# Edge terms on row groups, and four steps moved: n_h, the degrees' turn, a tap step and the first loads

## The chip, the cores and the metric

The kernel runs on one core of one Trainium2 chip. A core has TensorE (matrix products, results into eight PSUM banks), VectorE, ScalarE, GpSimd and SyncE; the profile calls them PE (PEld for its weight loads), DVE, ACT, POOL and SP. The metric is the device time of one execution in microseconds; lower is better. All data is float32.

## The reference, cut to what matters

x holds 128 graphs of 128 nodes with 256 channels. Layer 0 normalizes x and clips it at zero (h), and passes h through a gated network; layer 1 is a graph convolution over the first 25 nodes in five groups. What the change touches, cut from the reference:

```python
h = bn2(conv1d_17(relu(bn1(conv1(h)))))            # 17 taps along the nodes
x_conv = relu(h + xc)
s = x @ w_se.T + b_se                              # 3 numbers per node
sq = sum(s * s, axis=-1)
dist = sq[:, :, None] + sq[:, None, :] - 2.0 * einsum('bnd,bmd->bnm', s, s)
A = exp(-dist) * mask                              # mask: the graph's adjacency
msg = relu(x @ w_msg.T + b_msg)
x_nmp = einsum('bnm,bmd->bnd', A, msg)
x_in = concatenate([x_conv, x_nmp], axis=-1)
gi = x_in @ w_ih.T + b_ih
gh = x @ w_hh.T + b_hh
r, z = sigmoid(gi_r + gh_r), sigmoid(gi_z + gh_z)
nn_ = tanh(gi_n + r * gh_n)
out = (1.0 - z) * nn_ + z * x
# layer 1, for each of five groups of nodes
norm_adj = dinv[:, :, None] * (adj + I) * dinv[:, None, :]     # dinv: degree ** -0.5
out = relu(norm_adj @ (x @ W) + b)                             # twice
```

## The kernel before, in words

Work goes in 32 blocks of four graphs (BB = 4; 512 columns).

**Front, 0 to about 495 us.** The 17-tap convolution is done by spectra. weight_spectra (L155) turns the taps w2 into spectra in four steps per set, eight sets in all. One step is sixteen products with only 17 rows each (L162): the taps lie in four groups that start at partitions 0, 32, 64 and 96, so four products stand on four different row groups of the array and write to four banks. some_spectra (L361) does one such step wherever it is called. head_load, head_stats, head_norm, head_turn (transposes to ht, L209), head_conv1 (L223) and head_spectra (L238) bring the blocks of x to their spectra. constants (L119) computes the batch-norm factors: small operations on VectorE with a power on GpSimd, a broadcast bnb (L133), four products with the identity that spread it over the partitions (L136), a ScalarE copy bnr (L137) and the scaling of the weights wc1 (L138), which head_conv1 needs. Up to L391 every engine takes its instructions in the order of the code (manual_schedule, L350); after that only GpSimd and, for a while, SyncE do. spectral (L282) multiplies the spectra.

**Gates, about 495 to 1800 us.** For each block, beside_gates(i) (L950) is a generator whose steps prepare block i: messages (L512, its last three columns are s, put into lr), conv_out (L493, gives xc), edge_terms (L535), edges (L547), x_nmp (L558, gives xn). gate_inputs (L580) forms the sums t that the gates' seven-product scheme needs: of xc and ht on GpSimd, of xn on VectorE. gates(i) (L593) then runs four units of seven steps: r (from ht, xc, xn: six records of TensorE a step), n_h (from ht alone: two records), n_n (xc, xn: four), z (six). After each step it calls step() (L991), which advances the degrees' generator, and in every odd turn the preparation of block i + 1, in the other turns layer 1.

**Edges.** lr holds for each of the four graphs of a block 32 columns, of which five are used: 2s, -1 and -sq on the left side, s, sq and 1 on the right, so that five products per pair of nodes give -dist. edge_terms transposes both sides (L539); graph b's five rows then stand at partitions 32b to 32b + 4. It copies the left side to lt on ScalarE (L541), and on VectorE writes the right side into rt, 512 columns wide, with a mask bm (L543) that leaves in graph b's 128 columns only b's rows. One product of 128 rows and 512 columns (L552) gives all four graphs' -dist in one bank; one exp (L554) and one multiplication with the adjacency (L555) follow.

**Degrees.** degrees (L690) sums the adjacency's rows on VectorE, takes the power -0.5 in several steps, and then transposes the factors (L723), copies them (L725) and stores them (L726) in dvf and dvk. back_loads (L741) and prepare (L807) load them again, broadcast, for layer 1.

**Before the first block** the preparation of block 0 is done alone (L983), then its gate_inputs, then the loop over the blocks (L987).

PSUM is one pool of eight banks (L90), and bank() takes the next. SyncE's queue and ScalarE's queue issue the loads and stores.

Of the kernel before, what the change touches and what calls it, by code (L numbers as in the profile page):

```python
# [8 lines left out]
F32 = mybir.dt.float32  # L9
# [8 lines left out]
BB = 4  # L18
# [56 lines left out]
def gnn_kernel(ctx: ExitStack, tc: tile.TileContext, io, out0: bass.AP, out1: bass.AP):  # L75
# [43 lines left out]
    def constants():  # L119

        for j, v0 in enumerate((V_BN1, V_BN2)):
# [11 lines left out]
        nc.vector.tensor_copy(bnb, bn[:, 0].rearrange("p q c -> p (q c)")[:, :, None].to_broadcast([P, 2 * C, P]))  # L133
        psb = bank()
# [4 lines left out]
        nc.vector.tensor_add(brz, vec[:, V_IH:V_IH + 4], vec[:, V_HH:V_HH + 4])  # L139

# [199 lines left out]
    with front as es:  # L340
# [7 lines left out]
        with ExitStack() as ws:  # L348
# [6 lines left out]
            todo = [(c, q) for c in range(C) for q in range(D // WCH)]  # L355
            head_load(xk, ahead, 0, nc.scalar)
            nc.sync.dma_start(gt, io["gt"])
            taps = [taps_load(wp, *todo[0], nc.sync, split=4)]
# [23 lines left out]
            constants()  # L382
            some_spectra()
            head_stats(hk, 1)
            some_spectra()
            head_norm(1)
# [54 lines left out]
    def load(i):  # L441
# [9 lines left out]
        for b in range(BB):  # L451
# [31 lines left out]

    bm = cst.tile([P, BB], F32)
    nc.gpsimd.memset(bm, 1.0)
    nc.gpsimd.affine_select(out=bm, in_=bm, compare_op=ALU.is_ge, fill=0.0, base=0,
                            pattern=[[-32, BB]], channel_multiplier=1)
    nc.gpsimd.affine_select(out=bm, in_=bm, compare_op=ALU.is_ge, fill=0.0, base=31,
                            pattern=[[32, BB]], channel_multiplier=-1)

# [44 lines left out]
    def edge_terms(i):  # L535

        ps = bank()
        for k in range(2):
            nc.tensor.transpose(ps[:, k * P:(k + 1) * P], lr[:, k].rearrange("p b r -> p (b r)"), ident)  # L539
        lt = wk.tile([P, P], F32, tag="lt", name="lt", bufs=2)  # L540
        nc.scalar.copy(lt, ps[:, :P])  # L541
        rt = wk.tile([P, BB, N], F32, tag="rt", name="rt", bufs=1)
        nc.vector.tensor_tensor(rt, ps[:, None, P:2 * P].to_broadcast([P, BB, N]),  # L543
                                bm[:, :, None].to_broadcast([P, BB, N]), op=ALU.mult)
        lrs[i] = lt, rt

    def edges(i):  # L547

        at, _, _ = loaded.pop(i)
        lt, rt = lrs.pop(i)  # L550
        pd = bank()
        nc.tensor.matmul(pd, lt, rt.rearrange("p b n -> p (b n)"), start=True, stop=True)  # L552
        e = wk.tile([P, BB, N], F32, tag="e", name="e", bufs=1)
        nc.scalar.activation(e.rearrange("p b n -> p (b n)"), pd, AF.Exp)  # L554
        nc.vector.tensor_mul(e, e, at)  # L555
# [24 lines left out]
    def gate_inputs(i):  # L580

        tt = []
# [570 lines left out]
```

## Time and profile before

| | |
|---|---|
| three executions | 1921.88, 1923.89, 1928.10 us; median 1923.89 |
| the profiled execution | 1930.41 us, its span 1928.7 us |
| TensorE busy | 1900.0 us, 99% of the span |
| TensorE's mean clock | 0.992 of full |
| VectorE, ScalarE, GpSimd busy | 1288.2, 712.2, 610.3 us |
| L552, the edge product | 32 of 128x512 |
| one block of the gates without layer 1 | 37.15 us (725.11 to 762.26 in the chain of waits) |

All rows under the first are of the one profiled execution. A product of float32 is two records in the profile (L552 has 64 records for 32 products). Products overlap, so a record's own length (0.59 us for L552) is longer than the time by which it moves the next one; the chain of waits shows that time. "<-" behind an idle time names what ended it. Clock is the share of full speed that TensorE was granted.

### The profile page before, as it was taken

The page shows a single profiled execution, that of the slowest core. Times are in us where ns is not written, and L with a number is a line of the kernel's source. Part 1 is how long each engine was busy: PE and PEld are TensorE (multiplying, and loading weights), DVE is VectorE, ACT ScalarE, POOL GpSimd, SP SyncE. Part 2 cuts the span into 40 slices and gives each one's busy share as a digit, 9 for nine tenths or more (in the row PEclk, how much of TensorE's full clock was granted, in tenths as well). Part 3 has the DMA queues.
Part 4 walks back from the last instruction along what each step waited for, and adds up shares of the span by engine and source line. Part 5 has one row for each costly group of instructions (what it writes and reads, how often), then busy time and mean ns, then how long its engine had stood idle before and what let it go on. Part 6 is the DMA issues. An engine that isn't in the chain of part 4 may idle for free.

```text
span 1928.7 us, 29906 instructions
## 1 busy us (share of the span) xinstructions
PE 1900.0 (99%) x10418; PEld 1654.8 (86%) x10418; DVE 1288.2 (67%) x3247; ACT 712.2 (37%) x1459; POOL 610.3 (32%) x681
## 2 busy tenths in 40 slices
PE   8999999999999999999999999999999999999998
PEld 7888888988788888888888888888888888888887
DVE  6566547854687777877665677777656677787643
ACT  4453114411333343343343443334343433334334
POOL 1012541256234333433322233433322233343300
PEclk9899999999999999999999999999999999999999
DMA  8686987369842333233234433233234533222135
GB/s 310 256 317 231 304 286 254 133 227 305 273 117 72 72 91 80 74 94 107 71 89 100 131 88 94 72 72 114 79 86 94 150 72 101 70 72 74 35 93 150
DMA packets 248869, 265.76 MB, mean 138 GB/s; under 512 B 106866, under 2 KB 223943, under 8 KB 244239
## 3 DMA queue, kind: packets, MB, share of 16 engines
q1 hardware_dynamic: 236783, 196.74, 36.6%
q10 hardware_dynamic: 11936, 67.11, 9.0%
q8 instruction: 83, 1.36, 0.3%
q14 instruction: 67, 0.55, 0.1%
HBM read 178.66 MB, written 85.14 MB: 137 GB/s over the span
## 4 chain that ended last, share of the span: by engine, by line
PE 88%; DMA 5%; DVE 4%; POOL 1%; issue 1%; ACT 1%; SPq 0%; ACTq 0%; POOLq 0%; DVEq 0%
PE bank L613 43%; PE bank L314 6%; PE bank L519 5%; PE bank L933 5%; PE bank L873 5%; PE bank L223 4%; PE bank L309 3%; PE bank L565 3%; PE bank L501 3%; PE bank L238 3%; PE bank L162 2%; PE bank L552 1%; PE bank L504 1%; DMA v<-vd 1%; PE bank L852 1%; PE bank L784 1%
## 5 line engine op out<-in xcount | busy, mean ns | idle before, releaser
L613 PE MATMUL bank<-t,sw 128*128 128x256 f32 x1152 | 291.1, 380 | 0.0
L626 POOL TENSOR_TENSOR u<-u,m 128x256 f32<-128x256 f32 x128 | 92.8, 725 | 594.2 <-ACT m L624 524.6
L613 PEld LDWEIGHTS bank<-t,sw 128*128 128x128 f32 x1152 | 215.7, 190 | 29.7 <-issue 2.3
L613 PE MATMUL bank<-t,wih 128*128 128x256 f32 x768 | 197.2, 379 | 0.0
L613 PEld LDWEIGHTS bank<-t,wih 128*128 128x128 f32 x768 | 143.4, 190 | 19.3 <-issue 0.5
L306 POOL TENSOR_TENSOR vs<-v 128x512 f32<-128x512 f32 x78 | 101.4, 1320 | 115.8 <-DMA v<-vd 54.1
L223 PE MATMUL bank<-wc,ht 128*128 128x256 f32 x512 | 121.0, 389 | 1.7 <-ACT ht L210 1.6
L519 PE MATMUL bank<-wms,ht 128*128 128x259 f32 x512 | 122.3, 381 | 0.0
L613 PE MATMUL bank<-t,whh 128*128 128x256 f32 x384 | 114.9, 381 | 0.0
L613 PE MATMUL bank<-xc,wih 128*128 128x256 f32 x384 | 114.7, 380 | 0.0
L933 PE MATMUL bank<-w,hh 128*125 128x256 f32 (+9 forms) x480 | 113.5, 380 | 1.0 <-DVE hh L878 1.0
L613 PE MATMUL bank<-xn,wih 128*128 128x256 f32 x384 | 114.3, 379 | 0.1
L223 PEld LDWEIGHTS bank<-wc,ht 128*128 128x128 f32 x512 | 97.8, 196 | 16.6 <-ACT ht L210 3.6
L613 PE MATMUL bank<-ht,whh 128*128 128x256 f32 x384 | 110.3, 381 | 0.0
L519 PEld LDWEIGHTS bank<-wms,ht 128*128 128x128 f32 x512 | 97.2, 190 | 14.6
L873 PE MATMUL bank<-ax,w 128*128 128x500 f32 (+8 forms) x416 | 107.0, 396 | 0.3 <-DMA w<-in_w_dram 0.3
L631 DVE TENSOR_TENSOR u<-bank,u 128x256 f32<-128x256 f32 x128 | 53.7, 419 | 73.6 <-PE bank L613 73.6
L193 POOL TENSOR_TENSOR rs<-ve,mhalf 128x4 f32<-128x4 f32 x32 | 32.3, 1008 | 222.3 <-DVE ve L191 222.3
L523 ACT ACTIVATE msg<-msg 128x512 f32<-128x512 f32 x64 | 40.3, 630 | 168.2 <-DVE msg L520 162.2
L304 DVE SCALAR_TENSOR_TENSOR s<-X 128x256 f32<-128x256 f32 x78 | 49.0, 631 | 80.0 <-PE bank L314 79.8
L933 PEld LDWEIGHTS bank<-w,hh 128*125 128x125 f32 (+9 forms) x480 | 84.2, 177 | 19.3 <-DVE hh L878 1.4
L653 ACT ACTIVATE nn<-nn,vec 128x512 f32<-128x512 f32 x64 | 46.2, 722 | 129.6 <-DVE nn L652 129.6
(191 smaller groups left out, 4287.4 us busy)
## 6 DMA issues: line engine op xcount, KB each, us to landing
v<-vd SPq DMA_DIRECT2D x80, 512.0 KB
vd<-sp ACTq DMA_DIRECT2D x8, 2560.0 KB
yd<-ys ACTq DMA_DIRECT2D x40, 512.0 KB
w<-in_w_dram SPq DMA_DIRECT2D x40, 512.0 KB
htd<-ht ACTq DMA_DIRECT2D x32, 512.0 KB
ht<-htd SPq DMA_DIRECT2D x32, 512.0 KB
ym<-yd SPq DMA_DIRECT2D x32, 512.0 KB
xt<-in_xT_dram SPq DMA_DIRECT2D x32, 512.0 KB
```

Source lines behind the costliest of these rows:

```text
L223: nc.tensor.matmul(pv[:, bb, :], ht[:, c, b * N:(b + 1) * N], wc1[:, c, :], start=c == 0, stop=c == C - 1)
L238: nc.tensor.matmul(ps[:, bb * 2 * LW:(bb + 1) * 2 * LW], h1[:, 2 * h + bb, c * P:(c + 1) * P], fd, start=True, stop=True)
L306: nc.gpsimd.tensor_tensor(vs, vr, vi, op=ALU.add)
L309: nc.tensor.matmul(p1[:, :D], a[:, c], vs[:, c], start=c == 0, stop=c == C - 1)
L314: nc.tensor.matmul(ps[:, k * D:(k + 1) * D], u[:, c], w[:, c], start=c == 0, stop=c == C - 1)
L501: nc.tensor.matmul(ps[:, b * N:(b + 1) * N], ym[:, b, o * P:(o + 1) * P], idm, start=b == 0, stop=False)
L519: nc.tensor.matmul(ps[:, :D + 3], ht[:, c, b * N:(b + 1) * N], wms[:, c, :], start=c == 0, stop=c == C - 1)
L565: nc.tensor.matmul(ps[:, b * N:(b + 1) * N], msg[:, b, c * P:(c + 1) * P], e[:, b, :], start=True, stop=True)
L613: nc.tensor.matmul(ps, w, d, start=n == 0, stop=n == len(pairs) - 1)
L626: nc.gpsimd.tensor_tensor(got["u4"], got["u2"], got["m5"], op=ALU.add)
L873: nc.tensor.matmul(pv[:, q - q0, :], w1s[k5 + g][:, c, q * P:(q + 1) * P], xv[:, c], start=c == 0, stop=c == C - 1)
L933: nc.tensor.matmul(ps[:n1, :D], hh[:, q, at:at + n1], w2s[k5 + g][:, q, :], start=q == 0, stop=q == HID // P - 1)
```

## The change

1. **Edges.** rt and the mask bm go. edge_terms copies both transposed sides in one ScalarE copy (lt, now 2 x 128 columns). edges makes four products, each with the five rows of one graph at partitions 32b and 128 columns, into four banks; exp is taken four times over 128 columns, and the multiplication with the adjacency twice over two graphs.
2. **First block's n_h.** For block 0 the preparation stops when edges is done. The sums of ht and xc are formed, and gates(0) begins with the n_h unit. Behind its sixth step the rest of the preparation (x_nmp) and the sums of xn follow. In the other units of block 0 the preparation of block 1 advances on two turns of three instead of every odd turn. n_h's steps in block 0 don't call step(), so the degrees aren't advanced in them. Other blocks keep their order.
3. **Degrees.** Between the factors and their transposes the generator yields eight times instead of three.
4. **Norms' constants.** constants becomes a generator with two halts: one behind bnb, one at the end. Between them stand two steps of the spectra and head_stats of block 1.
5. **First loads.** gt is issued from ScalarE's queue ahead of block 0 of x; SyncE's queue begins with the four loads of the first taps.

```diff
@@ -118,6 +118,6 @@
 
     def constants():
         for j, v0 in enumerate((V_BN1, V_BN2)):
             g, b, m, v = (vec[:, v0 + 2 * q:v0 + 2 * q + 2] for q in range(4))
             sc, sh = bn[:, j, 0, :], bn[:, j, 1, :]
@@ -131,12 +132,14 @@
 
         bnb = hc.tile([P, 2 * C, P], F32, name="bnb")
         nc.vector.tensor_copy(bnb, bn[:, 0].rearrange("p q c -> p (q c)")[:, :, None].to_broadcast([P, 2 * C, P]))
+        yield
         psb = bank()
         for q in range(2 * C):
             nc.tensor.matmul(psb[:, q * P:(q + 1) * P], bnb[:, q, :], ident, start=True, stop=True)
         nc.scalar.copy(bnr.rearrange("p q d -> p (q d)"), psb)
         nc.vector.tensor_mul(wc1, wc1, bnr[:, 0:1, :].to_broadcast([P, C, D]))
         nc.vector.tensor_add(brz, vec[:, V_IH:V_IH + 4], vec[:, V_HH:V_HH + 4])
+        yield
 
     fw = cst.tile([P, 5], F32)
 
@@ -353,9 +356,9 @@
             wp = ws.enter_context(tc.tile_pool(name="wp", bufs=1))
             ahead = 5
             todo = [(c, q) for c in range(C) for q in range(D // WCH)]
+            nc.scalar.dma_start(gt, io["gt"])
+            taps = [taps_load(wp, *todo[0], nc.sync, split=4)]
             head_load(xk, ahead, 0, nc.scalar)
-            nc.sync.dma_start(gt, io["gt"])
-            taps = [taps_load(wp, *todo[0], nc.sync, split=4)]
             spectra = []
 
             def some_spectra(k=1):
@@ -379,10 +382,12 @@
             head_norm(0)
             some_spectra()
             head_turn(hk, 0)
-            constants()
+            consts = constants()
+            next(consts)
             some_spectra()
             head_stats(hk, 1)
             some_spectra()
+            next(consts)
             head_norm(1)
             head_stats(hk, 2)
             some_spectra()
@@ -479,14 +484,6 @@
     nb2 = cst.tile([P, 5, C], F32)
     nc.vector.tensor_mul(nb2, vec[:, V_B2:V_B2 + 5 * C].rearrange("p (g c) -> p g c", c=C),
                          nw[:, :, None].to_broadcast([P, 5, C]))
-    bm = cst.tile([P, BB], F32)
-    nc.gpsimd.memset(bm, 1.0)
-    nc.gpsimd.affine_select(out=bm, in_=bm, compare_op=ALU.is_ge, fill=0.0, base=0,
-                            pattern=[[-32, BB]], channel_multiplier=1)
-    nc.gpsimd.affine_select(out=bm, in_=bm, compare_op=ALU.is_ge, fill=0.0, base=31,
-                            pattern=[[32, BB]], channel_multiplier=-1)
 
     A_s, xcs, xns, ts, msgs, outs, lrs, xts = ({} for _ in range(8))
 
@@ -537,22 +534,23 @@
         ps = bank()
         for k in range(2):
             nc.tensor.transpose(ps[:, k * P:(k + 1) * P], lr[:, k].rearrange("p b r -> p (b r)"), ident)
-        lt = wk.tile([P, P], F32, tag="lt", name="lt", bufs=2)
-        nc.scalar.copy(lt, ps[:, :P])
-        rt = wk.tile([P, BB, N], F32, tag="rt", name="rt", bufs=1)
-        nc.vector.tensor_tensor(rt, ps[:, None, P:2 * P].to_broadcast([P, BB, N]),
-                                bm[:, :, None].to_broadcast([P, BB, N]), op=ALU.mult)
-        lrs[i] = lt, rt
+        lt = wk.tile([P, 2, P], F32, tag="lt", name="lt", bufs=2)
+        nc.scalar.copy(lt.rearrange("p k n -> p (k n)"), ps[:, :2 * P])
+        lrs[i] = lt
 
     def edges(i):
 
         at, _, _ = loaded.pop(i)
-        lt, rt = lrs.pop(i)
-        pd = bank()
-        nc.tensor.matmul(pd, lt, rt.rearrange("p b n -> p (b n)"), start=True, stop=True)
+        lt = lrs.pop(i)
+        pd = [bank() for _ in range(BB)]
+        for b in range(BB):
+            g = slice(32 * b, 32 * b + 5)
+            nc.tensor.matmul(pd[b][:, :N], lt[g, 0, :], lt[g, 1, :], start=True, stop=True)
         e = wk.tile([P, BB, N], F32, tag="e", name="e", bufs=1)
-        nc.scalar.activation(e.rearrange("p b n -> p (b n)"), pd, AF.Exp)
-        nc.vector.tensor_mul(e, e, at)
+        for b in range(BB):
+            nc.scalar.activation(e[:, b, :], pd[b][:, :N], AF.Exp)
+            if b % 2:
+                nc.vector.tensor_mul(e[:, b - 1:b + 1, :], e[:, b - 1:b + 1, :], at[:, b - 1:b + 1, :])
         A_s[i] = e
 
     def x_nmp(i):
@@ -577,30 +575,31 @@
 
         return d[:, 0, :H], d[:, 0, H:], d[:, 1, :H], d[:, 1, H:]
 
-    def gate_inputs(i):
-
-        tt = []
-        for k, (d, eng) in enumerate(((xcs[i], nc.gpsimd), (xns[i], nc.vector), (hts[i], nc.gpsimd))):
+    def gate_inputs(i, which=(0, 1, 2)):
+
+        tt = ts.setdefault(i, {})
+        for k in which:
+            d, eng = ((xcs, nc.gpsimd), (xns, nc.vector), (hts, nc.gpsimd))[k]
+            d = d[i]
             t = wk.tile([P, 4, H], F32, tag=f"t{k}", name=f"t{k}")
             b11, b12, b21, b22 = quarters(d)
             eng.tensor_tensor(t[:, 0], b12, b11, op=ALU.subtract)
             eng.tensor_tensor(t[:, 1], b22, t[:, 0], op=ALU.subtract)
             eng.tensor_tensor(t[:, 2], b22, b12, op=ALU.subtract)
             eng.tensor_tensor(t[:, 3], t[:, 1], b21, op=ALU.subtract)
-            tt.append(t)
-        ts[i] = tt
-
-    def gates(i, between, nxt):
-
-
-
-        ht, ins, tt = hts.pop(i), (xcs.pop(i), xns.pop(i)), ts.pop(i)
-        ins = ins + (ht,)
+            tt[k] = t
+
+    def gates(i, between, nxt, ahead=None):
+
+
+
+        ht, xc, tt = hts.pop(i), xcs.pop(i), ts[i]
+        ins = [xc, None, ht]
 
         def small(name):
             return wk.tile([P, H], F32, tag=name, name=name, bufs=2)
 
-        def unit(g, pairs, dst, order, hook=None):
+        def unit(g, pairs, dst, order, hook=None, between=between):
             got = {}
             for j in order:
                 ps = bank()[:, :H]
@@ -638,11 +637,16 @@
 
         o = wk.tile([P, C, T], F32, tag="o", name="o", bufs=2)
         r = o
+        nh = wk.tile([P, C, T], F32, tag="z", name="nh", bufs=1)
+        if ahead:
+
+            unit(2, (2,), nh, (1, 2, 6, 5, 3, 7, 4), between=ahead)
+        ins[1] = xns.pop(i)
         unit(0, (2, 0, 1), r, (1, 2, 6, 5, 3, 7, 4))
         for q in range(C):
             nc.scalar.activation(r[:, q, :], r[:, q, :], AF.Sigmoid, bias=brz[:, q:q + 1])
-        nh = wk.tile([P, C, T], F32, tag="z", name="nh", bufs=1)
-        unit(2, (2,), nh, (1, 2, 6, 5, 3, 7, 4))
+        if not ahead:
+            unit(2, (2,), nh, (1, 2, 6, 5, 3, 7, 4))
         for q in range(C):
             nc.vector.scalar_tensor_tensor(r[:, q, :], nh[:, q, :], vec[:, V_HH + 4 + q:V_HH + 5 + q], r[:, q, :],
                                            op0=ALU.add, op1=ALU.mult)
@@ -716,7 +720,7 @@
         nc.vector.tensor_scalar(t, t, -0.5, 1.5, op0=ALU.mult, op1=ALU.add)
         nc.vector.tensor_mul(y, y, t)
         nc.vector.tensor_sub(dinv, y, zero)
-        for _ in range(3):
+        for _ in range(8):
             yield
         for c0, c1, d in ((F0, K0, dvf), (K0, E0, dvk)):
             ps = bank()
@@ -980,9 +984,20 @@
     load(0)
     load(1)
     degs = degrees(*degree_loads())
-    for _ in beside_gates(0):
-        pass
-    gate_inputs(0)
+    begin = beside_gates(0)
+    while 0 not in A_s:
+        next(begin)
+    gate_inputs(0, (2, 0))
+    held = [6]
+
+    def sums_ahead():
+
+        held[0] -= 1
+        if held[0] == 0:
+            for _ in begin:
+                pass
+            gate_inputs(0, (1,))
+
     layer1s = []
     for i in range(NBLK):
         first = beside_gates(i + 1)
@@ -992,7 +1007,7 @@
 
             next(degs, None)
             turn[0] += 1
-            if turn[0] % 2 and next(first, STOP) is not STOP:
+            if (turn[0] % 2 if i else turn[0] % 3) and next(first, STOP) is not STOP:
                 return
             for _ in range(2 if i == NBLK - 1 else 1):
                 while layer1s and next(layer1s[0], STOP) is STOP:
@@ -1009,7 +1024,7 @@
             if i + 1 < NBLK:
                 gate_inputs(i + 1)
 
-        gates(i, step, nxt)
+        gates(i, step, nxt, None if i else sums_ahead)
         for k in range(len(PARTS)):
             if i * BB == first_of[k + 1]:
                 layer1s.append(layer1(k))
```

## The prediction

> **What bounds the kernel now.** I read the totals first: TensorE leads with 99%.
>
> ```profile
> PE 1900.0 (99%) x10418; PEld 1654.8 (86%) x10418; DVE 1288.2 (67%) x3247; ACT 712.2 (37%) x1459; POOL 610.3 (32%) x681
> ```
>
> An average hides stages, so next the busy time by stretch (columns: length, then busy time of PE, weight loads, VectorE, ScalarE, GpSimd, then clock and DMA).
>
> ```profile
> 495.00:508.00 13.00, 10.82 (x58) 8.97 (x58) 6.58 (x18) 4.04 (x7) 6.09 (x8) 0.90 0.83 223
> 508.00:530.00 22.00, 19.61 (x95) 16.23 (x94) 19.40 (x54) 9.76 (x17) 2.31 (x3) 0.97 0.95 300
> 530.00:550.00 20.00, 20.00 (x96) 17.60 (x95) 13.64 (x35) 4.52 (x9) 5.71 (x7) 0.93 0.47 131
> 577.00:1810.00 1233.00, 1233.00 (x6198) 1075.15 (x6197) 880.83 (x2112) 467.93 (x842) 431.40 (x505) 1.00 0.34 88
> ```
>
> From 577 to 1810 us TensorE has no idle time at all: a microsecond taken from its queue there is a microsecond off the end, as long as nobody else becomes late. Around 500 us, where block 0 of the gates starts, it isn't so: 2.2 of 13 and 2.4 of 22 us are idle, and from 508 to 530 VectorE is busy for 19.4 of 22.
>
> The chain of one steady block (start, length, what) shows the edge product on the path with its neighbours:
>
> ```profile
> 751.09 0.89 PE bank L501 x8
> 751.98 0.43 PE bank L504 x2
> 752.42 0.86 PE bank L613 x4
> 753.28 0.86 PE bank L552 x2
> 754.14 0.86 PE bank L613 x4
> ```
>
> An f32 product counts as two records, so the 128x512 product of L552 takes 0.86 us a block, and a full-array product of 128 columns (L501) 0.89/8 = 0.11 us a record.
>
> TensorE's own timeline shows the idle spells that the other edits aim at (in brackets):
>
> ```profile
> 501.64 1.04 PE L552 MATMUL bank<-rt,lt 128*128 128x512 f32 x2
> 504.82 3.21 PE L565 MATMUL bank<-e,msg 128*128 128x128 f32 x16 [2.13 <-DVE e L555]
> ...
> 528.33 0.42 PE L723 MATMUL bank<-ident,dinv 128*53 128x128 f32 x2 [2.32 <-DVE dinv L718]
> ```
>
> ```profile
> 5.84 3.72 PE L162 MATMUL bank<-gt,w 17*128 17x80 f32 x64 [5.84 <-DMA w<-in_w2t_dram]
> 9.49 1.98 PE L209 MATMUL bank<-ident,ln 128*128 128x128 f32 x8
> 13.86 2.05 PE L136 MATMUL bank<-ident,bnb 128*128 128x128 f32 x8 [2.39 <-DVE bnb L133]
> 15.84 5.42 PE L162 MATMUL bank<-gt,w 17*128 17x80 f32 x96
> ```
>
> Both idle spells near 500 us are followed by slow products: L565's sixteen records take 3.21 us where eight take 0.89 in the steady block.
>
> **What the Trainium skill says.** "TensorE: Matmul & The Clock Gate", Part 3 (packing small matmuls): products on different 32-row groups run at once, four of K=32 measured 3.07 times faster than in turn. The front of this kernel agrees: the weight spectra (17 rows in four row groups) do 32 records in 1.06 us, 33 ns each, where a full-array record of 128 columns takes 111. "TensorEngine Tiling (Array Packing)", Key Properties: a change of tiling mode drains the array. The trace agrees and gives the price below. The same page, Gotcha 1: different row tiles need different PSUM banks, hence the four banks here. The clock page's Part 1: idleness halves the array's clock for windows of about 3.4 us; the clock of 0.90, 0.97 and 0.93 in the three stretches above says the same (1.3, 0.7 and 1.4 us lost).
>
> **Part 1, edge terms on row groups.** Removed per block: the 0.86 us product, VectorE's masked copy rt (L543, 0.674 us) and, once, GpSimd's mask (0.10 + 0.20 + 0.27 us near 1 and 9 us, in idle time: nothing). Added: four products of 5 rows and 128 columns, a ScalarE copy of 256 columns instead of 128 (about 0.36, as L616's 256, against 0.265), four exps of 128 columns instead of one of 512, VectorE's product in two halves.
>
> TensorE's new time comes from the front, where spectra stand between full-array work:
>
> ```profile
> 120.07 3.45 PE bank L223 x16
> 123.53 1.06 PE bank L162 x32
> 124.59 1.02 PE bank L209 x8
> ...
> 130.96 3.65 PE bank L223 x16
> ```
>
> A round of four row groups needs two passes. A pass of 128 columns took 0.111 us in the full array, so I take 2 x 0.111 = 0.22 for a round. The 32 records are four rounds, 0.89; the 0.17 over is the switch in. The switch out is 3.65 - 3.45 = 0.20 (L223 behind spectra against L223 behind full-array work). One visit: 0.22 + 0.17 + 0.20 = 0.59 us. Saved: 0.86 - 0.59 = 0.27 a block. 128 columns are more than the spectra's 80, so a drain can be up to 48 columns longer (0.04); and the bank wait below may cost 0.1, of which I count a little. I take 0.22; bounds 0.13 and 0.27, nothing if the round doesn't overlap (rival D). Times 31 blocks (block 0 waits there anyway): **6.8 us**, 4 to 8.4.
>
> What hides the rest: exp's table load ends at 755.52 and exp runs to 756.13 in the block above. Four exps of about 0.27 each (0.265 for the 128-column copy) end near 756.6; VectorE's second half (about 0.4) then ends near 757.1, earlier than today's 757.61, since it need not come in one piece. x_nmp starts at 758.58, or 758.3 if TensorE is 0.25 ahead: covered. Banks are less roomy: of the eight, four now wait for exp. The products behind edges (two of n_h, L784, n_h's last) take four others, all read by 754.3; the next one, n_n's first, comes at 755.99 - 0.25 = 755.74, and if it gets the bank of the first exp, free at 755.8, it waits 0.1. Unknown cost: 0 to 0.14 a block.
>
> **Part 2, n_h ahead of r in block 0.** Today edges is followed by 2.13 us idle (exp, then VectorE), x_nmp at half clock and r. Now six n_h steps (2 records of 0.216: 0.43 each, 2.6 us together) stand in between; their inputs exist, since GpSimd finished ht's sums at 498.2. x_nmp would run 504.8 to 506.6, n_h's last step to 507.0, then r. Today r starts at 507.82 with n_h's 3.0 us still to come: 3.8 us gained, 4.3 with the clock. But VectorE stood still until the first degree table landed at 510.29 and its sum ended at 511.84; only then came xn's second half and r's second step at 512.45:
>
> ```profile
> 503.86 0.90 DVE L555 TENSOR_TENSOR e<-e,at 128x512 f32<-128x512 f32 x1 [1.27 <-ACT e L554]
> 510.31 1.53 DVE L694 TENSOR_REDUCE dinv<-dga 128x53 f32<-128x1325 f32 x1 [5.55 <-DMA dga<-in_adjF_dram]
> ```
>
> That landing doesn't move. If r's second step still waits for it, the gain is n_h's work alone: **3.0 us**. If n_h's five VectorE reads (0.42 each) are queued behind that sum too, 2.1 of it goes. Bounds 0.5 and 4.3. Block 1's steps run on two of three turns instead of one of two, with 21 turns instead of 28: 14 against 14, and they need 11.
>
> **Part 3, the degrees' turn later.** The two transposes, their ScalarE copies and the two stores on SP (0.24 and 0.32 us of issue at 529) move from the 11th to the 16th turn, that is, from n_h into z, some 10 us. The dinv they wait for comes from VectorE at 528.27 and is not later. So the 2.32 us idle go, and with them the half-speed time (530.38: two records in 1.06 instead of 0.59), 1.4 us: 3.7 at most. What is late next is VectorE itself (19.4 of 22): its backlog may hold edges or x_nmp of block 1. I take **3.0**, bounds 0 and 3.7. SP's broadcast loads of the factors stand behind the stores (dce at 531.99, first dck at 535.30): they slide with them, and what is queued behind them on SP too; dce is first used by L789 at 571.45, so 10 us fit. VectorE's L811/L812, which wait for dck and nt until 549, slide as well; they cost 0.26 us of TensorE idle at 572.72 today.
>
> **Part 4, the start.** gt goes from SP to ScalarE's queue ahead of the first block of x: SP's taps issue at 0.81 instead of 1.26, x at about 1.28 instead of 0.81. The first products start up to 0.45 earlier, but the chain x, statistics, norm, transposes (5.05 to 9.49) may come 0.47 later; as the transposes end nearer 11.8 than 11.4, this part gives nothing by itself. Then two spectra steps (32 records each; at this place 5.42/96 x 32 = 1.8 us) run where 2.39 us were idle; then L136 (2.05), one step (1.8), conv1. So conv1 starts at 11.8 + 3.6 + 2.05 + 1.8 = 19.3 instead of 21.20: **1.9 us**. wc1's product moves behind head_stats of block 1 (2.3 us of VectorE, its input issued at 5.42): about 18.4, in time. Bounds: -0.5, if x's lag passes on, and 4, if the clock also rises a window sooner. Cover later in the front: TensorE waits 1.82 us for a tap load at 68.70, issued when a set of spectra ends, so it shifts along.
>
> **Sum.** 6.8 + 3.0 + 3.0 + 1.9 = 14.7 us. Against the profiled execution: 1930.4 (span 1928.7 and 1.7 around it) to 1915.7. That execution is 6.5 us above the median of the runs shown, so for the median I subtract the same from 1923.9: 1909.2, say **1909**.
>
> **Rivals.** B, *banks*: the four banks and four exps make TensorE wait behind edges. For: all eight banks are in use at 755.3 by my count; one exp more in the way costs 0.27, which is the whole saving. Against: four other banks come first, and free. Then only 7.9 us remain: 1916. C, *VectorE keeps the opening*: for it stands 19.4 of 22 us. Parts 2 and 3 shrink to 1.5 together with part 4 reduced to nothing: 8.3 off, 1915.6. D, *the slower side: the four products don't stand together.* Outside the front the order isn't written out: L466, in the code behind the front, runs at 23.6 us. If n_h products get between the four (because a bank isn't free at planning), each of them is a visit of its own: 4 x 0.59 - 0.86 = 1.5 us a block, 46 in 31 blocks, less 7.9: 1962. With two visits the loss is 0.32 x 31 = 9.9, net +2; so it decides from the second visit on. The same mechanism covers products that don't overlap: eight passes in turn are 0.89 + 0.37, +0.4 a block, net +4.5. Against D: all four depend on one copy, and stand one after another in the code.
>
> **Chances.** Main case 0.54 (1909), B 0.19, C 0.19, D 0.08. Low end: 8.4 + 4.3 + 3.7 + 4 = 20.4 off, 1903. High end 1919 holds B and C with some spread; D and the tails are left out. 0.3% is 5.8 us, about what a measurement of this kernel can tell from no change: faster is below 1918.1. Main 0.96 of its chance, B 0.70, C 0.72: 0.52 + 0.13 + 0.14 = 0.79. Slower is most of D: 0.07. Same: 0.14.
>
> **What would show it.** Part 1: one visit of eight records per block with 0.59 us to the next product's start, no idle before n_n's first step, and the steady block at 36.93 instead of 37.15 us (725.11 to 762.26 in the chain). Part 2: no idle ahead of L565 in block 0, r's second step still near 512. Part 3: no wait at L723. Part 4: conv1 first at 19.3. Wrong: row-group records in several places of a block (D), a wait on exp before an L613 product (B), or VectorE as the releaser of new TensorE waits from 505 to 550 (C).

## The result and the profile after

| | before | after |
|---|---|---|
| median of 7 executions each | 1927.08 us (1921.88 to 1928.27) | 1917.82 us (1913.61 to 1920.39) |
| ratio after to before | | 0.9955, 95% interval 0.9939 to 0.9971 |
| the profiled execution, its span | 1930.41, 1928.7 us | 1919.48, 1917.7 us |

The kernel became 9.3 us faster; the forecast was 14.7. The median of before is 3.2 us higher than that of the three executions shown with the forecast, so of the 8.6 us between 1909.2 and 1917.8 about 3.2 are the base and 5.4 the effect.

Totals of the kernel after:

```profile
PE 1890.3 (99%) x10610; PEld 1646.4 (86%) x10610; DVE 1303.9 (68%) x3247; ACT 720.5 (38%) x1555; POOL 609.1 (32%) x678
```

Line numbers are now those of the kernel after: the products of edges are L548, exp L551, the gates' products L612, the degrees' transposes L727, their stores L730, the loads of dck L811, and VectorE's two operations that use them L815 and L816.

**The steady block is as forecast.** The chain of waits in a block without layer 1:

```profile
745.46 0.89 PE bank L498 x8
746.35 0.43 PE bank L501 x2
746.79 0.86 PE bank L612 x4
747.65 0.43 PE bank L548 x8
748.08 1.06 PE bank L612 x4
749.14 0.72 PE bank L788 x4
```

The eight records of edges stand in one piece. They take 0.43 us, and the gates' four records behind them 1.06 instead of 0.86: a visit (the way into the row groups, the products and the way out) costs 0.63, where the forecast had 0.59. The block is 36.93 us (719.47 to 756.40) instead of 37.15, exactly as forecast.

**Around 500 us it is not.** Busy time by stretch (length, then PE, weight loads, VectorE, ScalarE, GpSimd, clock, DMA):

```profile
495.00:508.00 13.00, 10.62 (x66) 8.96 (x64) 4.81 (x9) 4.03 (x11) 4.41 (x6) 1.00 0.93 280
508.00:530.00 22.00, 20.79 (x100) 17.78 (x101) 20.71 (x57) 10.36 (x18) 2.66 (x3) 0.85 0.85 254
530.00:550.00 20.00, 20.00 (x100) 17.66 (x100) 17.29 (x36) 6.48 (x12) 8.57 (x11) 1.00 0.43 119
550.00:572.00 22.00, 20.63 (x107) 17.33 (x106) 14.73 (x50) 8.47 (x18) 4.62 (x6) 0.92 0.52 118
```

Before, TensorE worked through 530 to 550 at a clock of 0.93, and through all but 0.26 us of 550 to 577 at full clock. Now 550 to 572 has 1.4 us of idle time and a clock of 0.92, which is 0.08 x 22 = 1.8 us more. TensorE's timeline names the places:

```profile
509.21 1.22 PE L612 MATMUL bank<-xn,wih 128*128 128x256 f32 x2 [3.58 <-DVE xn L566]
...
558.68 0.70 PE L612 MATMUL bank<-t,sw 128*128 128x256 f32 x2 [0.67 <-DVE u L504]
559.21 0.69 PE L612 MATMUL bank<-t,whh 128*128 128x256 f32 x2
559.84 0.49 PE L548 MATMUL bank<-lt 5*128 5x128 f32 x4
561.02 0.56 PE L548 MATMUL bank<-lt 5*128 5x128 f32 x4 [0.70 <-ACT m L615]
```

The wait at the degrees' transposes is gone, as forecast. A wait of 3.58 us at r's second step is there, and half a clock from 508.0 to 514.8. In block 1, near 560 us, TensorE waits twice: for VectorE's u, and in the middle of the edges for a bank that ScalarE's copy m had to free. The clock halves again from 562.6 to 566.0. VectorE's timeline shows what it stood in front of:

```profile
507.02 1.53 DVE L698 TENSOR_REDUCE dinv<-dga 128x53 f32<-128x1325 f32 x1 [5.18 <-DMA dga<-in_adjF_dram]
...
557.67 0.29 DVE L816 TENSOR_TENSOR nt<-nt,dck 125x125 f32<-125x125 f32 x1 [3.13 <-DMA dck<-dvk]
557.88 0.74 DVE L504 SCALAR_TENSOR_TENSOR u<-bank,bn,ht 128x512 f32<-128x512 f32 x1
558.54 0.28 DVE L816 TENSOR_TENSOR nt<-nt,dck 125x125 f32<-125x125 f32 x1
558.73 0.42 DVE L630 TENSOR_TENSOR u<-bank,u 128x256 f32<-128x256 f32 x1
```

At 557.67 VectorE had stood for 3.13 us in front of L816, an operation of layer 1, whose products are not due in block 1; behind it waited L504 and L630, which TensorE does need. L816 waited for dck, the factors that the degrees' turn stores. SP's queue (start, length of the issue) shows why they are late:

```profile
535.30 0.25 SPq L730 DMA_DIRECT2D dvf<-dvt  x1
535.64 0.32 SPq L730 DMA_DIRECT2D dvk<-dvt  x1
...
543.22 3.04 SPq L811 DMA_DIRECT2D dck<-dvk  x3
546.32 0.72 SPq L809 DMA_DIRECT2D nt<-in_adjN_dram  x2
550.15 0.64 SPq L763 DMA_DIRECT2D out_dram<-xt  x1
550.88 0.61 SPq L765 DMA_DIRECT2D xf<-xl  x1
551.60 1.37 SPq L811 DMA_DIRECT2D dck<-dvk  x3
```

The stores are at 535.3 (before: 529), and three of the dck loads got behind block 0's output stores, to 551.6; before, eleven dck loads were issued ahead of these stores, here six. The place in the queue isn't the only bound: dck has three buffers, and the one that the load at 551.60 fills was read by an L816 until 551.0. The chain of waits shows this load landing 6.05 us after its issue; that ended VectorE's wait.

**The start.** TensorE's timeline:

```profile
3.90 3.72 PE L165 MATMUL bank<-gt,w 17*128 17x80 f32 x64 [3.90 <-DMA gt<-in_gt_dram]
10.25 2.25 PE L212 MATMUL bank<-ident,ln 128*128 128x128 f32 x8 [2.63 <-issue]
12.43 3.72 PE L165 MATMUL bank<-gt,w 17*128 17x80 f32 x64
16.07 2.08 PE L138 MATMUL bank<-ident,bnb 128*128 128x128 f32 x8
18.08 2.01 PE L165 MATMUL bank<-gt,w 17*128 17x80 f32 x32
20.02 5.31 PE L226 MATMUL bank<-wc,ht 128*128 128x256 f32 x16
```

The 2.39 us wait for bnb is gone, but the transposes come at 10.25 instead of 9.49, and conv1 starts at 20.02: 1.2 us gained there, where 1.9 was forecast. The place scatters: in the nine traces with both edits of the start conv1 begins between 19.9 and 21.5 us.

**A ruler for the experiments.** Times from the first message product of one block to that of another compare the traces part by part. From block 3 to block 31 every trace with the old edges shows 1176.68 or 1176.69 us, every one with the new edges 1170.34 or 1170.35: 6.34 less over 28 blocks, 0.226 a block. The opening, from block 0 to block 3, was 93.4 us before and is 94.2 after. The time to block 0, 0 to about 490 us, scatters by 6 to 7 us between traces with the same start.

### The profile page after: what moved, and what is told of

It is laid out like the page before. It is cut to its first block, busy times and chain, and to the rows that moved or that the text cites. A ratio compares the mean times of both kernels' runs of the same rounds, so it can differ in the third digit from the quotient of the medians.

```text
span 1917.7 us, 30432 instructions
## 1 busy us (share of the span) xinstructions
PE 1890.3 (99%) x10610; PEld 1646.4 (86%) x10610; DVE 1303.9 (68%) x3247; ACT 720.5 (38%) x1555; POOL 609.1 (32%) x678
## 3 DMA queue, kind: packets, MB, share of 16 engines
q1 hardware_dynamic: 236639, 196.70, 36.9%
## 4 chain that ended last, share of the span: by engine, by line
PE 88%; DMA 4%; DVE 4%; issue 2%; ACT 1%; POOL 1%; SPq 0%; ACTq 0%; POOLq 0%; DVEq 0%
PE bank L612 45%; PE bank L317 6%; PE bank L516 5%; PE bank L937 5%; PE bank L877 5%; PE bank L226 4%; PE bank L312 3%; PE bank L563 3%; PE bank L498 3%; PE bank L241 3%; PE bank L165 2%; PE bank L501 1%; PE bank L788 1%; PE bank L856 1%; DMA v<-vd 1%
## 5 line engine op out<-in xcount | busy, mean ns | idle before, releaser
L612 PE MATMUL bank<-t,sw 128*128 128x256 f32 x1152 | 291.6, 380 | 0.7 <-DVE u L504 0.7
L612 PEld LDWEIGHTS bank<-t,sw 128*128 128x128 f32 x1152 | 215.8, 191 | 31.1 <-issue 2.3
L612 PE MATMUL bank<-t,wih 128*128 128x256 f32 x768 | 197.2, 379 | 0.0
L612 PEld LDWEIGHTS bank<-t,wih 128*128 128x128 f32 x768 | 143.4, 190 | 19.3 <-issue 0.5
L612 PE MATMUL bank<-xn,wih 128*128 128x256 f32 x384 | 114.9, 381 | 3.6 <-DVE xn L566 3.6
L612 PE MATMUL bank<-t,whh 128*128 128x256 f32 x384 | 115.0, 381 | 0.0
L612 PE MATMUL bank<-xc,wih 128*128 128x256 f32 x384 | 114.8, 381 | 0.0
L516 PEld LDWEIGHTS bank<-wms,ht 128*128 128x128 f32 x512 | 98.3, 192 | 15.1
L612 PE MATMUL bank<-ht,whh 128*128 128x256 f32 x384 | 109.9, 380 | 0.0
L630 DVE TENSOR_TENSOR u<-bank,u 128x256 f32<-128x256 f32 x128 | 53.7, 420 | 73.6 <-PE bank L612 73.5
```

What stands on the lines that cost most here:

```text
L516: nc.tensor.matmul(ps[:, :D + 3], ht[:, c, b * N:(b + 1) * N], wms[:, c, :], start=c == 0, stop=c == C - 1)
L612: nc.tensor.matmul(ps, w, d, start=n == 0, stop=n == len(pairs) - 1)
```

## The experiments

After the first comparison there were two theories. **Q, late factors:** parts 1, 2 and 4 work; the late turn makes dck late, VectorE's queue stands in order in front of it, and TensorE pays in block 1. **R, the opening is VectorE's:** whatever is moved, VectorE from 500 to 530 us gives the time back elsewhere. The late turn is part 3 of the prediction, eight yields; the early turn is the three yields of before. Times below are differences from the kernel before in the same series, worked out from the ratio: (ratio - 1) x 1928 us.

**Parts alone, on the kernel before.** Edges alone (part 1 of the diff):

> The kernel before with the edge change alone (row groups, four exps, no rt and no mask). Theory 1 (the edge step gives what was forecast, the opening gives nothing): 0.22 us a steady block, 36.93 instead of 37.15, 6.8 us in all, ratio to before 0.9965. Rival (the edge step gives less, for instance because its waits come back as other waits in blocks with layer 1, and the opening gives its 6 us): 3 us or less, ratio 0.9985 or more.

Measured: 1920.72 us, ratio 0.996 (0.9946 to 0.9974), -7.7 us. The opening is 95.8 us, longer than before, with a longer wait at the transposes. TensorE reached them 1.4 us earlier after block 0's first message, and dinv came 1.4 us later; why dinv was later isn't shown:

```profile
527.49 0.49 PE L716 MATMUL bank<-ident,dinv 128*53 128x128 f32 x2 [5.13 <-DVE dinv L711]
```

The start alone (parts 4 and 5 of the diff):

> The kernel before with the two edits of the start alone (first taps first in their queue, two tap steps amid the norms' constants). Forecast: 1.9 us. Theory 1: 1.2 to 2.5 us, ratio about 0.999; conv1 first near 20.0 us instead of 21.2, and the rest of the 5.5 us by which the front of the changed kernel was shorter comes from the clock, so it differs from run to run. Rival: all 5.5 us belong to the edits, ratio 0.997.

Measured: 1924.39 us, ratio 0.998 (0.9969 to 0.9991), -3.9 us; conv1 at 20.04. The ratio lies midway between the two expectations (0.999 and 0.997), and its interval holds both.

Block 0's n_h ahead of r alone (gate_inputs in two calls, gates with ahead, sums_ahead; part 2 of the diff):

> The kernel before with part 2 alone (block 0's n_h ahead of r, the degrees turned at their 11th turn as before). Theory Q: part 2 gives its 3 to 5 us by itself, because with n_h gone from behind r the 11th turn falls after VectorE has dinv, so the 2.3 us wait at the transposes shrinks to under 1 us: 1922 to 1924 beside 1927 before, ratio 0.9975 to 0.9985. Rival (parts 2 and 3 need each other: without the late turn TensorE reaches the transposes 3 us earlier and waits the more for dinv): the wait at the transposes grows to 4 or 5 us and the time is within 1 us of before.

Measured: 1921.5 us, ratio 0.9973 (0.9962 to 0.9985), -5.2 us, a little more than Q expected. The opening is 88.8 us, 4.6 less than before, and no half clock falls in it. The wait at the transposes, with the early turn:

```profile
529.38 0.42 PE L729 MATMUL bank<-ident,dinv 128*53 128x128 f32 x2 [1.41 <-DVE dinv L724]
```

It shrank from 2.32 to 1.41 us by part 2 alone, less than the fall to under 1 us that Q expected. The turn is counted in steps: with n_h's short steps gone from behind r, the 11th turn falls among longer ones, at 36.7 us from block 0's first message instead of 33.3. So parts 2 and 3 were meant to save the same wait.

The late turn alone:

```diff
-        for _ in range(3):
+        for _ in range(8):
             yield
```

> The kernel before with part 3 alone (eight turns instead of three between the degrees' sums and their transposes; n_h behind r). Theory Q: the wait at the transposes (2.3 us in before) goes, but the stores and dck come some 8 to 10 us later, so that VectorE stands in front of L811/L812 in block 1 and TensorE waits there with a half-clock window: between 1 us faster and 4 us slower than before. Rival (my forecast's part 3): 2.3 to 3.7 us faster than before, no new wait in block 1.

Measured: 1924.42 us, ratio 0.9991 (0.998 to 1.0001), -1.7 us. With n_h still behind r, the five more turns include n_h's short steps: the transposes come at 39.4 us from block 0's first message, not at 45.1 as in after, and dck is issued from 43.3 instead of 48.7. Block 1 shows only a wait of 0.26 us, as before. So Q's wait for dck in block 1 did not come, and the gain of 2.3 to 3.7 us that the rival expected isn't shown either. No loss shows for the late turn by itself; it needs part 2 to become one.

**The change without the late turn** (eight back to three in the kernel after):

> The changed kernel with the degrees' transposes back at the 11th turn (three yields). Theory 1 (the later turn delays the broadcast loads of the factors, and VectorE stands before them in block 1): the waits of TensorE at 558 and 561 us and the half clock behind them vanish, 3 us; a wait of up to 1.5 us at the transposes comes back; 1.5 to 3 us faster than the changed kernel, about 1915.5. Rival (the later turn is worth its 3 us as forecast): the wait of 2.3 us and the half clock at the transposes come back, about 1921.

Measured: 1912.53 us, ratio 0.9918 (0.9901 to 0.9935), -15.8 us; a second series (as the baseline of the last experiments) gave

> The kernel after with the early turn (3) again, now on one chip beside the two kernels that follow, as their baseline. Its ratio to before was 0.9918: expected 0.991 to 0.993. All theories expect the same of it; what tells them apart is the distance to the next two.

1913.36 us, 0.9917 (0.9898 to 0.9936). The direction is that of theory 1; the gain over after, 7.1 us by the ratios, is larger than the 1.5 to 3 it expected. This kernel is faster than before and than after: its intervals end at 0.9935 and 0.9936, after's begins at 0.9939. Its opening is 87.5 us. Its waits:

```profile
507.05 0.70 PE L612 MATMUL bank<-xn,wih 128*128 128x256 f32 x2 [1.54 <-DVE xn L566]
...
524.87 0.39 PE L727 MATMUL bank<-ident,dinv 128*53 128x128 f32 x2 [0.61 <-ACT e L551]
...
555.17 0.60 PE L612 MATMUL bank<-t,sw 128*128 128x256 f32 x2
555.61 0.59 PE L612 MATMUL bank<-t,whh 128*128 128x256 f32 x2
556.13 0.50 PE L548 MATMUL bank<-lt 5*128 5x128 f32 x8
```

Of the wait that part 3 was to remove 0.61 us is left, and it ends with ScalarE's exp (e), no longer with dinv. In block 1 there is no wait, and the eight records of the edges stand in one piece again. From block 2's first message to block 3's it takes 36.9 us where after takes 41.1.

**Is it dck?** The early turn changes much in VectorE's order. So the late turn was kept, and only L815 and L816 were taken from block 1's queue:

```diff
+            with tc.issue_after(read3[-1].ins):
                 nc.vector.tensor_add(nt[:n, :n], nt[:n, :n], ident[:n, :n])
                 nc.vector.tensor_mul(nt[:n, :n], nt[:n, :n], dc[:n, :n])
```

> The kernel after with one edit: the two VectorE operations of prepare that read nt and dck (L815, L816) are queued behind the newest read of r's third product, so that they no longer stand in VectorE's queue in block 1, ahead of what block 1 needs; TensorE's order is that of after. Theory Q (the late turn costs because the stores, and with them SP's load of dck behind block 0's output stores, come later, and VectorE stands 3.1 us in order in front of L816): the wait at L816 near 557 us is gone, block 1's products (gates at 558.7, the split edges visit at 561) start without the 0.7 us waits, no half clock from 562 to 566, and the kernel is 3 to 6 us faster than after: 1912 to 1915. Rival R (the late turn costs by its own place: the degrees' transposes and copies now fall where TensorE and ScalarE are short of slack, or the loss against the early turn is the half clock at 508 to 515 alone, which this edit doesn't touch): within 1.5 us of after, 1916.5 to 1919.

Measured: 1911.88 us, ratio 0.9927 (0.9905 to 0.9949), -14.1 us, against -8.7 for after. The stretch from block 2 to block 3 is 36.9 us, no wait falls in it, and the clock is back, as Q expected:

```profile
550.00:572.00 22.00, 22.00 (x123) 19.43 (x123) 15.02 (x35) 8.90 (x19) 6.36 (x8) 1.00 0.32 85
```

TensorE's order is the same as in after, and the stores come as late (45.3 us from block 0's first message, after 45.8). So the loss in block 1 is VectorE's wait in order for dck, shown by removal. The edit takes more away than the wait, though: the two operations now first run at 913.6 us, and with them go all dck loads of block 1 but the first three. Whether that alone gives time is asked by the control, the same edit with the early turn:

> The kernel after with the early turn (3) and L815/L816 queued off block 1: the control for the edit that queues them. Theory Q: with the early turn dck lands in time, so that this edit gives nothing: within 2 us of the early turn alone, whose ratio was 0.9918, so 0.991 to 0.993. Rival (the two operations cost VectorE time in block 1 whether dck is late or not, 21 pairs of 0.2 to 0.3 us): 3 us faster than that, ratio 0.990 or less.

Measured: 1915.07 us, ratio 0.9931 (0.9916 to 0.9946): no gain over 0.9918, as Q expects where dck is early. So the absence of these operations and loads shows no gain of its own.

**Can the first degree sum be moved?** VectorE waits 2.6 to 8.6 us in front of it (L698 in after) in the traces with the old order, while xn's copy stands behind. First it was begun at the fifth turn of r and queued behind a read of r, with the late turn:

```diff
-            next(degs, None)
+            if i == 0 and turn[0] == 5:
+                with tc.issue_after(read3[-1].ins):
+                    next(degs)
+            elif i or turn[0] > 5:
+                next(degs, None)
```

> The changed kernel with the degrees begun at the fifth turn of the r unit and their first sum queued on VectorE behind r's third product. Theory 1 (VectorE's in-order wait for the first degree table, 5.2 us to 507, holds xn's second half, and so TensorE for 3.6 us and then half a clock window or more): no wait of TensorE at 505 to 509 us, 3.6 to 6 us faster than the changed kernel, 1912 to 1914. Rival (the table's landing bounds the opening wherever the sum stands, or something else is late next): the wait moves, within 1 us of the changed kernel.

Measured: 1922.24 us, ratio 0.9967 (0.9951 to 0.9983), -6.4 us. Theory 1's gain over after did not come. The wait for xn is gone, as it expected, and block 0 is 5.2 us shorter than in after (block 0's first message to block 2's: 47.9 against 53.1). But the degrees then began later, the stores came at 47.6 us from the first message, and from block 2's first message to block 3's it took 44.8 us (41.1 in after):

```profile
557.21 0.80 PE L548 MATMUL bank<-lt 5*128 5x128 f32 x4 [2.80 <-DVE o L635]
```

VectorE's o waited behind a 2.36 us stand for dck. Of the 5.2 us that block 0 had gained, 3.8 were lost there, the same way as in after.

Then the sum was queued directly behind xn's sums (issue_after on the last of them), with the early turn and L815, L816 moved:

> The kernel after with the old turn (3 instead of 8), the first degree sum queued on VectorE behind xn's four sums, and prepare's L815/L816 queued as in the run with after's late turn. Theory Q: against the old turn alone (1912.5) the 1.5 us wait for xn at r's second step goes, and the waits left are those at the transposes, which grow by as much as the sum is later (1.5 us) unless a turn's work hides it: 1910 to 1913, 0 to 2.5 us faster than the old turn alone. Rival (VectorE is full from 508 to 530, so a wait removed in one place comes back in another, with a half-clock window of about 1.7 us): 1913 to 1917.

Measured: 1919.04 us, ratio 0.9964 (0.9953 to 0.9976), -6.9 us: here Q's expectation was wrong. The rival had the mechanism, and its range ended at 1917. The wait for xn is gone, and the wait at the transposes is longer than in any other trace:

```profile
531.33 0.64 PE L731 MATMUL bank<-ident,dinv 128*53 128x128 f32 x2 [5.36 <-DVE dinv L726]
```

The clock of 530 to 550 is 0.83. The first sum itself was not late: it began 15.1 us after block 0's first message, in the control above 15.8. Yet dinv was ready some 3 us later than in the control; what held the steps between isn't shown. With the late turn in the same kernel:

> After's late turn (8), the first degree sum queued on VectorE behind xn's four sums, and L815/L816 queued off block 1: the run before this one (early turn) with the turn late again. Theory Q: the 5.4 us wait at the transposes goes (they come some 8 us later, when dinv is there), and no wait for dck can come back; left is at most a wait of 1 to 2.5 us for lr or o on VectorE: 8 to 10 us faster than the same kernel with the early turn, 1908 to 1912, ratio 0.990 to 0.993. Rival (what is late moves on along VectorE's queue): a wait of 2 us or more on a VectorE tile other than dinv, with a half-clock window: 1913 to 1918.

Measured: 1913.25 us, ratio 0.9931 (0.9914 to 0.9947); 6.4 us faster than with the early turn, where Q expected 8 to 10, and the opening is 87.2 us. No wait of 2 us or more is left, so the rival's mechanism did not come. So the late turn does what it was forecast to do where dinv is late and dck can't hurt, and the result is not better than the early turn alone. R holds to this extent: with n_h ahead, the degrees early, early or late with L815 and L816 moved, and late behind xn all end at an opening of 87.2 to 89.1 us.

**What separates the openings is the half clock.** With n_h ahead, the eight traces in that range have no half clock in the opening. The other three, 92.7 to 94.2 us (after, the sum behind r's third product, and the sum behind xn with the early turn), have 6.8 to 10.2 us of it.

**The start.** Only the constants split, and only gt moved, each on the kernel before:

> The kernel before with only the norms' constants split around two steps of spectra (gt stays on SP). My forecast's part 4: nearly all of the start's gain is here, since two steps of spectra fill the 2.39 us in which TensorE waited for bnb: conv1 near 19.6 to 19.9, ratio 0.998 to 0.999, as with both start edits (0.998). Rival (the start's gain is the first taps' earlier issue): conv1 within 0.4 us of before's 21.2 and a ratio of 0.9995 or more.

> The kernel before with only gt moved from SP's queue to ScalarE's ahead of x. My forecast's part 4: TensorE begins earlier (3.9 instead of 5.8 us was seen with both), but the transposes of the first x come up to 0.5 us later, and the constants' wait stays, so conv1 is within 0.5 us of 21.2 and the time within 1 us of before, ratio 0.9995 to 1.0005. Rival (an earlier begin alone moves the clock's first windows): 2 us or more faster, ratio under 0.999.

Measured: 1927.29 us, 0.9998 (0.9987 to 1.0008), and 1929.11 us, 1.0005 (0.9991 to 1.0019). The split alone brings conv1 to 18.85 (2.35 us earlier), the moved gt to 22.37 (1.2 later); neither changes the time clear of noise. Expected were a ratio of 0.998 to 0.999 for the first and conv1 within 0.5 us of 21.2 for the second; neither came. Two places where lead can go, in the kernel with the split alone:

```profile
18.85 6.57 PE L225 MATMUL bank<-wc,ht 128*128 128x256 f32 x16
...
231.07 1.10 PE L316 MATMUL bank<-v,s 128*128 128x256 f32 x4 [2.98 <-issue]
...
255.47 1.10 PE L316 MATMUL bank<-v,s 128*128 128x256 f32 x4 [3.44 <-issue]
```

The first sixteen records of conv1 take 6.57 us, before 5.19, at full speed 3.45 (the prediction's L223). In every trace they begin by starting 0.43 us apart and then change to 0.22, so the excess is half speed. In the split kernel that lasts until 24.6 us, and before until 24.3, so 1.4 of the 2.35 us goes at once in this pair. But the change comes anywhere from 22.6 to 26.3 us in the seventeen traces, and 1.3 us apart in the two traces of the change with the early turn, so the loss in this pair may be scatter. Waits from 224 to 258 us come in all seventeen traces, 0.4 to 6.4 us in sum, without order in the edits. Both edits once more, in the kernel with the early turn, beside its baseline of 0.9917:

> The early-turn kernel with gt back on SP's queue, that is, without the half of the start edits that made TensorE's first transposes 0.9 us later; the constants are still split. Theory S (the start edits give their 4 us only together): 3 to 4 us slower than the baseline of this call. Rival T (the start's lead is lost in the waits for streamed tables from 200 to 260 us, and the 4 us of the two together were a scatter of the medians): within 1.5 us of it, conv1 near 18.9.

> The early-turn kernel without both start edits: the edges and block 0's n_h ahead alone. If the parts add and the start is worth the 4 us measured alone: 4 us slower than the baseline, ratio 0.994. Rival T: within 1.5 us of the baseline, ratio 0.992 to 0.9925, although conv1 is 1.2 us later.

Measured: 1914.69 us, 0.9917 (0.9899 to 0.9935), and 1915.73 us, 0.9932 (0.9912 to 0.9951). No gain shows for moving gt. In these traces conv1 starts at 18.78 and 20.96, and in their baseline at 20.92, not 1.2 us ahead of the kernel without the edits. The start as a whole is worth 2.9 us here and 3.9 alone, each uncertain by 2 us or more; the split alone gave 0.4. Block 0's first message comes at 491.7 us in the mean of the five traces with the old start and at 488.8 in the nine with both edits, but each group spreads over 6 to 7 us. Between 0 and some 4 us it stays open.

## Why the forecast was wrong

**The parts add up, without the late turn.** Edges -7.7, n_h -5.2, start -3.9: together -16.8. The three in one kernel measured -15.8 and -16.0, and edges with n_h alone -13.1 for -12.9 added. The whole change is at -8.7 in the same measure. So the late turn costs about 7 us (-8.7 against -15.8 and -16.0, each uncertain by about 3) where the forecast had it gain 3.0. The traces agree: the opening is 94.2 us in after and 87.5 with the early turn. Of these 6.7 us, 1.7 are more idle time (5.0 against 3.3) and 5.1 are half clock (10.2 us at half speed against none).

**Part 1** was right: 0.226 us a block for 0.22, one visit of eight records, no products between the four (rival D) in any trace with the new edges, and no wait in the steady blocks (rival B). Such a wait stands only near the opening: in the middle of the edges in block 1 of after and of the kernel with the sum behind r's third product, and probably in the 0.61 us at the transposes with the early turn, which end with exp. The visit costs 0.63, not 0.59, which the forecast's allowance of 0.05 covered.

**Part 2** was right in that the wait for e goes (2.13 us), and too small: 3.0 taken, bounds 0.5 to 4.3; the opening's trace shows 4.6, the medians 5.2 (interval 2.9 to 7.3). The term mis-sized is the clock: TensorE's idle time in the opening fell only from 4.8 to 4.0 us, and 3.4 us come from the 6.8 us of half clock that stay out. Half of that is the window behind the transposes, which the forecast gave to part 3 with the wait there. xn's wait stayed, as forecast, and its size scatters with the table's landing: VectorE's first degree sum began 14.9 to 18.3 us after block 0's first message in the traces where it kept its place. The two latest (17.5 and 18.3) have the late turn, but its other two (16.1 and 16.5) lie among the early ones. Whether that is the turn's doing isn't settled.

**Part 3 failed**, in two steps of its sum. The first is "So the 2.32 us idle go, and with them the half-speed time": with n_h ahead, only 0.61 us of that wait is left at the early turn, and no half clock follows, so there was little to gain. The second is "SP's broadcast loads of the factors stand behind the stores ...: they slide with them ... VectorE's L811/L812, which wait for dck and nt until 549, slide as well; they cost 0.26 us of TensorE idle at 572.72 today". The stores slid by 11.9 us from block 0's first message (33.9 to 45.8), as the forecast's "some 10 us" said. But L811/L812 (now L815/L816) did not slide: they kept their place in VectorE's queue, in block 1, and VectorE waited there for dck. And the 0.26 us was never dck's price: in before this wait is for e, the edges' product with the adjacency:

```profile
572.72 1.16 PE L565 MATMUL bank<-e,msg 128*128 128x128 f32 x8 [0.26 <-DVE e L555]
```

The forecast checked when dce is first used and put no price on a late dck, where its own reading of the queue (dck's loads stand behind the stores and slide with them) named who would be late. Measured in after: 4.2 us in block 1, of which 1.4 idle and 1.7 half clock (3.4 us of it); the rest, about 1 us, isn't placed.

The late turn's other 2.6 us in that trace (block 0's first message to block 2's: 53.1 against 50.6) stand with the long xn wait and its half clock. The kernel with L815 and L816 moved has such a wait too, 2.54 us, without a half clock behind it.

**Part 4** had its mechanism right at the place (two steps of spectra in the 2.39 us, conv1 earlier), and x's lag at 0.76 us was larger than the 0.47 it allowed for. Whether conv1's lead is the kernel's lead, as the sum took it, isn't settled: the split alone brought 2.35 us there and 0.4 in the time, with an interval from 1.5 us slower to 2.5 faster.

**Rival C**, VectorE keeps the opening, gave 1915.6 and lay nearer to the time than the main case; that is partly luck. It named the right engine, and the wait for xn at 509 us lies in its stretch of 505 to 550; but the place shown to cost most, 558 to 566 us, lies behind it, the cause is a late load, and that the start gives nothing isn't shown.

## What to carry to other kernels

When a step that produces something is delayed, look up every instruction that consumes it and ask whether it moves too: in an engine that works in order it keeps its place, and all that stands behind it waits. Two edits that aim at one wait save it once; cost the second against the kernel with the first. And count a delay in the steps it is made of: five more turns were 6.1 us with n_h behind r (33.3 to 39.4 from block 0's first message) and 9.6 with n_h ahead (35.5 to 45.1).

## What was not expected of the hardware

Half clock came in windows of 3.4 us or two of them together, 6.8. Near 500 to 560 us all five TensorE waits of 2.8 to 5.4 us had one during or right after them. Of the eleven waits of 2.1 to 2.6 us there, five had one (both in before) and six had none (2.54 and 2.43 us in the kernel with L815 and L816 moved). In after a window also followed two waits of 0.67 and 0.70 us. So the length of a single wait doesn't tell. Each window costs 1.7 us or more, half its length, as much as the edits studied here. In before the profile's clock reads 1.00 in the first 50 us although conv1's first products take 5.2 us where 3.45 is full speed; over all traces it is 5.0 to 6.6. And the scatter of single executions is large beside the stretches: from block 3 to block 31 all traces of a kind agree to 0.01 us, while before alone ranged from 1919.18 to 1935.57 us in 59 executions. The front has a part in it: its half-clock time was 3.4 to 20.5 us in the seventeen traces.
